# A Mamba stage whose first image is read before its weights

## The chip, the cores and the metric

The kernel runs on one core of a Trainium2 chip. Its engines work side by side, each through its own queue in order: TensorE (PE) multiplies matrices, VectorE (DVE) and GpSimd (POOL) work on tiles element by element, ScalarE (ACT) evaluates functions, and SyncE (SP) issues the DMA transfers between HBM and on-chip memory. Instructions on different engines wait for each other by semaphores. The metric is the device time of one execution in microseconds; lower is better. "Granted clock" is the share of TensorE's full clock that the throttle let through, by the profile.

## The reference, cut to what matters

Two layers, each added to its input: a Mamba block on group-normalised input, then an attention block on group-normalised input. The input x is 2 images of 256 channels with 64 x 64 positions, all float32. Layer 0, which the change is about:

```
x  = x + L0(gn(x))                      # gn: 32 groups of 8 channels, mean and variance over channels and all positions
yn = layernorm over channels * gamma + beta
xm, z = split(yn @ W_in.T)              # 512 each
u  = silu(causal conv of 4 taps (xm) + conv_b)
proj  = u @ W_xp.T                      # 16 for dt, 16 for B, 16 for C
dt = softplus(proj_dt @ W_dt.T + b_dt);  A = -exp(A_log)
h  = exp(dt A) h + (dt u) B             # scan over 4096 positions, 512 x 16 states
ym = (sum(h C) + u D) * silu(z)
y2 = ym @ W_out.T + yn
y3 = gelu(y2 @ W1.T + b1) @ W2.T + b2 + y2
```

The group norm needs the statistics of a whole image before the first of its positions can be normalised. Layer 1 is attention with 8 heads over 4096 positions; the change doesn't touch it.

## The kernel before

`conv_preact_kernel` loads a few constants, runs `mamba_stage` for both images, then `attention_block` for each. Within the Mamba stage an image is cut into 8 tiles of 512 positions (T), so there are 16 tiles: tiles 0 to 7 are the first image's, 8 to 15 the second's. An image tile is 128 partitions x 2 x 512 float32, which is 512 KB.

For each tile there are three parts. `front(i)` loads the tile into a buffer of the ring `yn` (L459), applies the group norm with the image's scales (L457), takes the mean over channels on PE, centres on DVE (L471), squares on ACT (L474), takes the variance on PE, then its inverse root on ACT (L479, L480), scales on DVE (L488) and shifts on ACT (L492). Four convolutions follow (`conv`): a projection on PE, a copy on ACT (L540), the taps as matmuls on PE, a silu on ACT (L536). Then come the projection to dt, B and C, and `softplus`. All these matmuls are recorded at L403, the line of a helper. The loop of `step` does the scan: 32 steps for each tile, with products on POOL and DVE and scans on DVE (L721). `back(i)` does the output projection (L599) with `w_out` and the two-layer perceptron with `w_1` and `w_2`.

The group norm's statistics come from `first(b, t)`: a load of an image tile into ring `h` (L315), and two `bn_stats` on DVE (L321), one for each half of the channels. Ring `h` has 5 buffers and is also that of the scan's steps. `group_norm(b, k)` aggregates (L412), averages over groups with two small matmuls by `gmat` (L403), and takes an inverse root on ACT by Ln and Exp (L424, L425). These and the front's inverse root need ACT's table "exp", the convolution's silu the table "silu"; a change of table is a load on ACT (L234). PSUM tiles of the front and of the group norm share the ring `mm` of 3 buffers.

The order of the stage's instructions is worked out by `Plan` when the kernel is built. Each task has an engine, a due time, a cost, and for DMAs a time to landing. Whenever an engine is free in the plan's time, the ready task with the lowest due (plus 6 when ACT's table would change) that finds buffers is put next. A task is only considered when its due is at most 24 (HORIZON) beyond the earliest due still unstarted:

```
if task.ready <= now and task.due <= dues[oldest].due + HORIZON:
    rank = (task.due + (SWITCH if task.tables and table not in task.tables else 0), task.at)
    if (best is None or rank < best[0]) and self.room(task, now):
```

That order is emitted under `tc.manual_schedule()`, so each engine's queue holds it as planned, however long things take on the chip. Tile i has its dues around 32 i: its front from 32 i - 46 (the load) over -39 (centring), -35 (scaling), -33 + 4k (the convolutions) to -12; its steps from 32 i on.

```
for b in range(IMAGES):
    for t in range(NT):
        first(b, t, -60 + 10 * b)
for b in range(IMAGES):
    for k in range(KC):
        group_norm(b, k, -48 + 10 * b)
```

Ahead of the plan stands the preparation: SP issues the loads of all weights and small vectors, in the order of the code (L334, L329, L341, L347, L349), then `perm`, `W_dt` and `pick` into the three buffers of ring `yn`. DVE works them into constants: `neg_a` (L359), `diag_d` (L364), `taps` (L369), `w_dt` (L379, L380) and `pick` (L383). The framework may change the order of these within the preparation.

Of the kernel before, what the change touches and what calls it, by code (L numbers as in the profile page):

```python
# [11 lines left out]
F32 = mybir.dt.float32  # L12
# [7 lines left out]
P = 128  # L20
# [3 lines left out]
D = 32  # L24
# [77 lines left out]
class Plan:  # L102
# [26 lines left out]
    def add(self, engine, due, cost, emit, reads=(), writes=(), tables=(), lands=0.0):  # L129


        task = Plan.Task()
        task.engine, task.due, task.cost, task.emit = engine, due, cost, emit
        task.tables, task.lands, task.at = tables, lands, len(self.tasks)
        deps = set()
        reads, writes = list(self.keys(reads)), list(self.keys(writes))
        for key in reads:
            deps.add(self.writer.get(key))
        for key in writes:
            deps.add(self.writer.get(key))  # L140
            deps.update(self.readers.get(key, ()))
        for key in reads:
            self.readers.setdefault(key, []).append(task)
        for key in writes:
            self.writer[key], self.readers[key] = task, []
        deps -= {None, task}
        task.deps, task.behind = len(deps), []
        task.ready, task.start = 0.0, None
        for dep in deps:
            dep.behind.append(task)  # L150
        task.bufs = list({id(b): b for b, _ in reads + writes}.values())
        for buf in task.bufs:
            if buf.ring and not buf.left:
                buf.turn = buf.ring.asked
                buf.ring.asked += 1
            buf.left += 1
        self.tasks.append(task)
# [89 lines left out]
def mamba_stage(ctx, tc, xs, stats_out, consts, w, outs):  # L247
# [12 lines left out]
    nc = tc.nc  # L260
    ident, gmat, lnmat, eps_t = consts
    IMAGES = len(xs)
    C, L = xs[0].shape
    KC = C // P
    NT = L // T
    DI = w["conv_w"].shape[0]
    KD = DI // P
    R = w["W_dtT"].shape[0]
    NP = w["W_xpT"].shape[1]
    N = (NP - R) // 2  # L270
    HID = w["W1T"].shape[1]
    KH = HID // P
# [6 lines left out]
    NS = LOW + NP  # L279

    wp = ctx.enter_context(tc.tile_pool(name="l0w", bufs=1))
# [4 lines left out]
    def ring(name, bufs, n=1, pool=None, rows=P, dtype=F32, free=False):  # L286
        return Ring(pool or sb, [rows, T] if n == 1 else [rows, n, T], name, bufs, dtype, free)

    mm = ring("mm", 3, pool=ps, free=True)
    r_yn, r_u, r_z = ring("yn", 3, KC), ring("u", KD + 1), ring("z", KD)  # L290
# [7 lines left out]
    r_h, r_y = ring("h", 5, 2), ring("y", 1, pool=ps)  # L298
# [5 lines left out]
    add = plan.add  # L304

    def image_tile(x, t):
        return x.rearrange("(k p) l -> p k l", p=P)[:, :, bass.ts(t, T)]


    stats_in = [wp.tile([P, KC, NT, nc.vector.BN_STATS_DIM], F32, name=f"stats_in{b}") for b in range(IMAGES)]  # L310
    stats_bufs = [Buf(parts=KC * NT, tile=s) for s in stats_in]

    def first(b, t, due):
        xt = Buf(r_h)
        add("SP", due, 0.8, lambda: nc.sync.dma_start(xt.tile, image_tile(xs[b], t)), [], [xt], lands=3.0)  # L315
        for k in range(KC):
            add(
                "DVE",
                due,
                0.7,  # L320
                lambda k=k: nc.vector.bn_stats(stats_in[b][:, k, t, :], xt.tile[:, k, :]),  # L321
                [xt],
                [stats_bufs[b][k * NT + t]],
            )


    def load_rows(name, src, k):
        t = wp.tile([P, k, src.shape[1]], F32, name=name)
        nc.sync.dma_start(t, src.rearrange("(k p) f -> p k f", p=P))  # L329
        return t  # L330

    def load_vec(name, src, k):
        t = wp.tile([P, k], F32, name=name)
        nc.sync.dma_start(t, src.rearrange("(k p) -> p k", p=P))  # L334
        return t

    gamma = load_vec("gamma", w["gamma"], KC)
    beta = load_vec("beta", w["beta"], KC)
    w_in = load_rows("w_in", w["W_inT"], KC)
    conv_w = wp.tile([P, KD, TAPS], F32, name="conv_w")  # L340
    nc.sync.dma_start(conv_w, w["conv_w"].rearrange("(k p) o t -> p k (o t)", p=P))  # L341
    conv_b = load_vec("conv_b", w["conv_b"], KD)
    w_xp = load_rows("w_xp", w["W_xpT"], KD)
    b_dt = load_vec("b_dt", w["b_dt"], KD)
    d_vec = load_vec("d_vec", w["D"], KD)
    neg_a = wp.tile([P, KD, QUAD, NQ], F32, name="neg_a")
    nc.sync.dma_start(neg_a, w["A_log"].rearrange("p (k j q) -> p k j q", k=KD, j=QUAD))  # L347
    sum4 = wp.tile([P, PQ], F32, name="sum4")
    nc.sync.dma_start(sum4, w["sum4"])  # L349
    w_out = load_rows("w_out", w["W_outT"], KD)  # L350
    w_1 = load_rows("w_1", w["W1T"], KC)
    b_1 = load_vec("b_1", w["b1"], KH)
    w_2 = load_rows("w_2", w["W2T"], KH)
    b_2 = load_vec("b_2", w["b2"], KC)


# [1 line left out]
    nc.scalar.activation(neg_a, neg_a, AF.Exp)  # L358
    nc.vector.tensor_scalar_mul(neg_a, neg_a, -1.0)  # L359
    diag_d = wp.tile([P, KD, P], F32, name="diag_d")  # L360
    perm = r_yn.make()[:, 0, 0:P]
    nc.sync.dma_start(perm, w["perm"])
    for k in range(KD):
        nc.vector.tensor_scalar_mul(diag_d[:, k, :], perm, d_vec[:, k : k + 1])  # L364

# [6 lines left out]
    w_dt = wp.tile([NS, 2, DI], F32R, name="w_dt")  # L372
    nc.gpsimd.memset(w_dt.bitcast(F32), 0.0)
    pick = wp.tile([NS, NQ, P], F32R, name="pick")
    w_dt32 = r_yn.make()[:R, 0, :]
    nc.sync.dma_start(w_dt32, w["W_dtT"])
    for row in (0, LOW):
        rows = slice(row, row + R)
        nc.vector.tensor_copy(w_dt[rows, 0, :], w_dt32)  # L379
        nc.vector.tensor_sub(w_dt[rows, 1, :], w_dt32, w_dt[rows, 0, :].bitcast(F32))  # L380
    pick32 = r_yn.make()[:NS, 0, :]
    nc.sync.dma_start(pick32, w["pick"])
    nc.vector.tensor_copy(pick.rearrange("r q p -> r (q p)"), pick32)  # L383

    projs = [wp.tile([NS, T], F32R, name=f"proj{i}") for i in range(2)]
    for t in projs:
        nc.gpsimd.memset(t.bitcast(F32), 0.0)
    r_proj.make = itertools.cycle(projs).__next__

# [9 lines left out]
    def matmul(out, pairs):  # L401
        for i, (lhsT, rhs) in enumerate(pairs):
            nc.tensor.matmul(out, lhsT=lhsT, rhs=rhs, start=(i == 0), stop=(i == len(pairs) - 1))  # L403

    def group_norm(b, k, due):

        s = Buf(r_gn)
        p1, p2 = Buf(mm), Buf(mm)
        out = scales_buf[b * KC + k]

        def aggregate():
            nc.vector.bn_aggr(s.tile[:, 0:2], stats_in[b][:, k, :, :].rearrange("p a s -> p (a s)"))  # L412

        def spread():


            nc.vector.tensor_copy(s.tile[:, 2:3], p1.tile[:, 0:1])
            nc.vector.tensor_sub(s.tile[:, 3:4], s.tile[:, 0:1], s.tile[:, 2:3])
            nc.vector.scalar_tensor_tensor(
                s.tile[:, 4:5], s.tile[:, 3:4], s.tile[:, 3:4], s.tile[:, 1:2], ALU.mult, ALU.add  # L420
            )

        def root():
            nc.scalar.activation(s.tile[:, 5:6], p2.tile[:, 0:1], AF.Ln, bias=eps_t)  # L424
            nc.scalar.activation(scales[:, b, k, 1:2], s.tile[:, 5:6], AF.Exp, scale=-0.5)  # L425

        def shift():
            nc.vector.scalar_tensor_tensor(
                scales[:, b, k, 0:1], s.tile[:, 2:3], -1.0, scales[:, b, k, 1:2], ALU.mult, ALU.mult
            )  # L430

        add("DVE", due, 0.4, aggregate, [stats_bufs[b][k * NT + t] for t in range(NT)], [s])
        add("PE", due, 0.4, lambda: matmul(p1.tile[:, 0:1], [(gmat, s.tile[:, 0:1])]), [s], [p1])
        add("DVE", due, 0.6, spread, [p1], [s])
        add("PE", due, 0.4, lambda: matmul(p2.tile[:, 0:1], [(gmat, s.tile[:, 4:5])]), [s], [p2])
        add("ACT", due, 0.6, root, [p2], [s, out], ("exp",))
        add("DVE", due, 0.2, shift, [s], [out])
# [325 lines left out]
            add("DVE", g + 2.5, 0.7, lambda: nc.vector.tensor_mul(d.z[k].tile, y.tile, d.z[k].tile), [y], [d.z[k]])  # L763

    for b in range(IMAGES):
        for t in range(NT):
            first(b, t, -60 + 10 * b)
    for b in range(IMAGES):
        for k in range(KC):
            group_norm(b, k, -48 + 10 * b)  # L770
    front(0)
    for i, d in enumerate(tiles):
        d.z, d.b, d.c, d.dt_rep, d.dtu_rep = [], [], [], {}, {}
# [482 lines left out]
```

## Time and profile before

| | us |
|---|---|
| median of 4 runs | 4627.26 (4626.51 to 4631.47) |
| the profiled execution | 4622.42 |
| its span, first to last instruction | 4620.6 |
| busy: PE, DVE, ACT, POOL | 4309.9, 3651.8, 3687.3, 3905.1 |
| first image load issued (L315, SP) | 15.91 |
| first and last of the 32 statistics (L321, DVE), starts | 22.8, 44.4 |
| first aggregation (L412, DVE) | 45.03 |
| first scaling in front 0 (L488, DVE) | 58.38 |
| first scan (L721, DVE) | 109.74 |

The granted clock over the span is 0.974. The page of the profile gives busy times over the whole span and in 40 slices; the timeline gives single instructions with their start and length in microseconds, and in brackets how long the engine stood idle before them and what ended that; "x10" after an instruction means that ten like it follow each other and are merged. A line with "SPq" is an instruction of SP's queue that issues a DMA: its length is the issue, not the transfer. The chain that ended last is found backwards from the last instruction, from each to what released it.

### The profile page before, as it was taken

How to read it: one execution, taken by the hardware profiler on the slowest of the kernel's cores; microseconds unless marked ns; L12 is line 12 of the kernel's file. 1: busy time of each engine (PE TensorE's matmuls, PEld its weight loads, DVE VectorE, ACT ScalarE, POOL GpSimd, SP SyncE). 2: the span in 40 equal slices, each digit the busy share in tenths (PEclk: the TensorE clock that was granted, in tenths of full speed). 3: DMA queues.
4: the chain of work that ended last, by engine and by line, in shares of the span. 5: the costliest groups of instructions: out<-in, count | busy, mean ns of one | idle time of the engine just before them, and what ended most of it. 6: DMA issues, size and time to landing. Idle time of an engine off the chain costs nothing.

```text
span 4620.6 us, 55923 instructions
## 1 busy us (share of the span) xinstructions
PE 4309.9 (93%) x18530; PEld 1569.5 (34%) x18530; DVE 3651.8 (79%) x3916; ACT 3687.3 (80%) x4860; POOL 3905.1 (85%) x2283
## 2 busy tenths in 40 slices
PE   4799899999999999888999999999989999999998
PEld 2233333333333333324333333333343333333332
DVE  3999999999999999964777767777747777777776
ACT  3788888888888888742888888888838888888887
POOL 1999999999999999960888888888818888888887
PEclk9899999999999999989999999999999999999999
DMA  5333333333333333308210140101081110401000
GB/s 174 105 111 110 103 122 121 122 124 124 124 124 123 111 119 124 114 33 266 66 44 17 26 99 19 26 17 26 10 266 33 44 26 19 99 17 26 23 25 8
DMA packets 162330, 379.67 MB, mean 82 GB/s; under 512 B 23408, under 2 KB 41584, under 8 KB 153840
## 3 DMA queue, kind: packets, MB, share of 16 engines
q1 hardware_dynamic: 162032, 376.03, 26.4%
q8 instruction: 147, 2.41, 0.2%
q14 instruction: 151, 1.24, 0.1%
HBM read 282.64 MB, written 93.32 MB: 81 GB/s over the span
## 4 chain that ended last, share of the span: by engine, by line
PE 64%; POOL 12%; DVE 10%; issue 6%; DMA 4%; ACT 3%; SPq 1%; POOLq 0%; DVEq 0%; ACTq 0%
PE s L963 27%; PE po L986 22%; PE mm L403 6%; DVE h L721 6%; POOL h L727 6%; POOL dbu L716 3%; PE y L753 2%; DMA xn<-x_dram 2%; PE mm L599 2%; PE mm L635 1%; PE s L887 1%; DVE bn L716 1%; PE bn L403 1%; ACT L234 1%; POOL lw L572 1%
## 5 line engine op out<-in xcount | busy, mean ns | idle before, releaser
L977 ACT ACTIVATE e<-s 128x1024 f32<-128x1024 f32 x2048 | 1987.6, 1023 | 284.5 <-PE s L963 281.7
L1007 DVE TENSOR_TENSOR acc<-acc,e 128x1024 f32<-128x1024 f32 x992 | 1220.0, 1230 | 566.4 <-ACT e L977 563.3
L1018 POOL TENSOR_TENSOR acc_p<-acc_p,e 128x1024 f32<-128x1024 f32 x544 | 1299.3, 2388 | 228.2 <-ACT e L977 214.8
L963 PE MATMUL s<-q,k 128*128 128x512 f32 x4096 | 1321.5, 436 | 12.9 <-ACT e L977 10.0
L727 POOL TENSOR_TENSOR h<-h,c 128x1024 f32<-128x1024 f32 x512 | 1205.7, 2369 | 16.3 <-ACT state L724 11.0
L986 PE MATMUL po<-e,v 128*32 128x512 f32 x8192 | 1093.8, 605 | 0.0
L963 PEld LDWEIGHTS s<-q,k 128*128 128x128 f32 x4096 | 615.8, 188 | 1131.5 <-ACT e L977 1123.0
L710 ACT ACTIVATE da<-dt_rep,neg_a 128x512 f32<-128x512 f32 x1024 | 691.7, 701 | 122.4 <-DVE h L721 100.9
L721 DVE TENSOR_TENSOR_SCAN h<-da,state,dbu 128x512 f32<-128x512 f32 x512 | 649.8, 1274 | 80.4 <-POOL dbu L716 70.9
L721 DVE TENSOR_TENSOR_SCAN h<-da,state,bn 128x512 f32<-128x512 f32 x512 | 647.5, 1265 | 13.7
L1016 POOL TENSOR_TENSOR acc_p<-acc_p,e 128x512 f32<-128x512 f32 x416 | 533.7, 1283 | 32.7 <-POOL acc_p L1018 0.2
L716 POOL TENSOR_TENSOR dbu<-dtu_rep,b 128x512 f32<-128x512 f32 x384 | 487.4, 1281 | 10.5 <-DMA dtu_rep<-dtu_dram 9.1
L234 ACT ACT_TABLE_LOAD x331 | 424.7, 1283 | 6.5 <-PEq L1246 0.7
L753 PE MATMUL y<-h,sum 128*32 128x512 f32 x2048 | 380.5, 641 | 41.3 <-POOL h L727 41.3
L403 PE MATMUL bn<-proj,pick 112*128 112x512 f32 x512 | 306.4, 614 | 118.8 <-DVE h L721 118.3
L716 DVE TENSOR_TENSOR bn<-dtu_rep,bn 128x512 f32<-128x512 f32 x512 | 348.7, 681 | 34.4 <-PE bn L403 17.2
L1009 POOL TENSOR_TENSOR acc_p<-e 128x1024 f32<-128x1024 f32 x32 | 76.4, 2388 | 270.6 <-ACT e L977 270.6
L986 PEld LDWEIGHTS po<-e,v 128*32 128x32 f32 x8192 | 161.6, 108 | 375.0 <-issue 361.7
L403 PE MATMUL mm<-yn,w_in 128*128 128x512 f32 x512 | 262.7, 638 | 10.0 <-ACT yn L492 4.5
L1015 DVE TENSOR_TENSOR acc<-acc,e 128x512 f32<-128x512 f32 x384 | 264.8, 690 | 0.0
L403 PE MATMUL mm<-xm,taps 128*128 128x512 f32 x512 | 235.6, 603 | 15.8 <-POOL xm L539 13.6
L403 PE MATMUL mm<-yn,w 128*128 128x512 f32 x512 | 239.1, 596 | 11.5 <-ACT z L587 10.3
(126 smaller groups left out, 3470.1 us busy)
## 6 DMA issues: line engine op xcount, KB each, us to landing
dt_rep<-dt_dram SPq DMA_DIRECT2D x128, 512.0 KB, 5.3
dtu_rep<-dtu_dram SPq DMA_DIRECT2D x128, 512.0 KB, 5.8
qk_dram<-halves SPq DMA_DIRECT2D x64, 512.0 KB, 5.7
q<-qk_dram SPq DMA_DIRECT2D x128, 256.0 KB, 4.7
k<-qk_dram SPq DMA_DIRECT2D x64, 512.0 KB, 7.4
b<-bc_dram SPq DMA_DIRECT2D x64, 256.0 KB, 3.0
c<-bc_dram SPq DMA_DIRECT2D x64, 256.0 KB, 4.0
dt_dram<-dt SPq DMA_DIRECT2D x64, 256.0 KB, 2.0
```

Source lines behind the costliest of these rows:

```text
L403: nc.tensor.matmul(out, lhsT=lhsT, rhs=rhs, start=(i == 0), stop=(i == len(pairs) - 1))
L710: nc.scalar.activation(da[j].tile, dt.tile[:, j, :], AF.Exp, scale=scale)
L716: engine.tensor_mul(out.tile, dtu.tile[:, j, :], rows.tile)
L721: nc.vector.tensor_tensor_scan(h.tile[:, j, :], da[j].tile, dbu.tile, initial, ALU.mult, ALU.add)
L727: nc.gpsimd.tensor_tensor(h.tile, h.tile, rows_c.tile.unsqueeze(1).to_broadcast([P, 2, T]), ALU.mult)
L753: nc.tensor.matmul(y.tile[j * PQ : (j + 1) * PQ, :], lhsT=sum4, rhs=pair[j // 2].h.tile[:, j % 2, :], start=False, stop=(qd == NQ - 1),)
L963: nc.tensor.matmul(ps[:, j, :], lhsT=keys[i // NT, kt][:, h, kj : kj + P], rhs=queries[i][:, h, :], start=True, stop=True,)
L977: nc.scalar.activation(e, d.s[half], AF.Exp, scale=SCALE)
L986: nc.tensor.matmul(tiles[i].po[h * D : (h + 1) * D, :], lhsT=v[:, c, g * P + h * D : g * P + (h + 1) * D], rhs=todo[s].e[h // 2][:, h % 2, :],
L1007: nc.vector.tensor_add(acc, acc, ea)
L1016: nc.gpsimd.tensor_add(acc_p[:, 1, :], acc_p[:, 1, :], eb[:, 1, :])
L1018: nc.gpsimd.tensor_add(acc_p, acc_p, eb)
```

## The change

The first image's statistics leave the plan. They are emitted directly, ahead of all weights: for each of the 8 tiles the load and its two `bn_stats`, in a scheduled block of their own. The second image's stay in the plan with due -30 instead of -50, and the group norms have dues -48 and -24 instead of -48 and -38.

The loads of the weights come in another order: those that the first front uses first, with `W_dt`, `pick` and `perm` among them rather than at the end; `w_in` moves behind the small convolution vectors. `W_dt` and `pick` now take the first two buffers of ring `yn` and `perm` the third. The three matrices that only `back` uses, `w_out`, `w_1` and `w_2` (512 KB, 1 MB and 1 MB), are loaded by a task of the plan on SP with due -20.

```diff
     def first(b, t, due):
         xt = Buf(r_h)
-        add("SP", due, 0.8, lambda: nc.sync.dma_start(xt.tile, image_tile(xs[b], t)), [], [xt], lands=3.0)
+        load = lambda: nc.sync.dma_start(xt.tile, image_tile(xs[b], t))
+        stats = lambda k: nc.vector.bn_stats(stats_in[b][:, k, t, :], xt.tile[:, k, :])
+        if b == 0:
+
+            xt.tile = r_h.make()
+            load()
+            for k in range(KC):
+                stats(k)
+            return
+        add("SP", due, 0.8, load, [], [xt], lands=3.0)
         for k in range(KC):
...
+            add("DVE", due, 0.7, lambda k=k: stats(k), [xt], [stats_bufs[b][k * NT + t]])
+
+    with tc.manual_schedule():
+        for t in range(NT):
+            first(0, t, 0)
...
     gamma = load_vec("gamma", w["gamma"], KC)
     beta = load_vec("beta", w["beta"], KC)
-    w_in = load_rows("w_in", w["W_inT"], KC)
     conv_w = wp.tile([P, KD, TAPS], F32, name="conv_w")
     nc.sync.dma_start(conv_w, w["conv_w"].rearrange("(k p) o t -> p k (o t)", p=P))
     conv_b = load_vec("conv_b", w["conv_b"], KD)
+    w_in = load_rows("w_in", w["W_inT"], KC)
     w_xp = load_rows("w_xp", w["W_xpT"], KD)
     b_dt = load_vec("b_dt", w["b_dt"], KD)
-    d_vec = load_vec("d_vec", w["D"], KD)
     neg_a = wp.tile([P, KD, QUAD, NQ], F32, name="neg_a")
     nc.sync.dma_start(neg_a, w["A_log"].rearrange("p (k j q) -> p k j q", k=KD, j=QUAD))
+    w_dt32 = r_yn.make()[:R, 0, :]
+    nc.sync.dma_start(w_dt32, w["W_dtT"])
+    pick32 = r_yn.make()[:NS, 0, :]
+    nc.sync.dma_start(pick32, w["pick"])
+    d_vec = load_vec("d_vec", w["D"], KD)
+    perm = r_yn.make()[:, 0, 0:P]
+    nc.sync.dma_start(perm, w["perm"])
     sum4 = wp.tile([P, PQ], F32, name="sum4")
     nc.sync.dma_start(sum4, w["sum4"])
-    w_out = load_rows("w_out", w["W_outT"], KD)
-    w_1 = load_rows("w_1", w["W1T"], KC)
     b_1 = load_vec("b_1", w["b1"], KH)
-    w_2 = load_rows("w_2", w["W2T"], KH)
     b_2 = load_vec("b_2", w["b2"], KC)
...
+    late_buf = Buf()
+
+    def load_late():
+        for tile_, name in ((w_out, "W_outT"), (w_1, "W1T"), (w_2, "W2T")):
+            nc.sync.dma_start(tile_, w[name].rearrange("(k p) f -> p k f", p=P))
...
     for b in range(IMAGES):
-        for t in range(NT):
-            first(b, t, -60 + 10 * b)
+        for t in range(NT if b else 0):
+            first(b, t, -30)
     for b in range(IMAGES):
         for k in range(KC):
-            group_norm(b, k, -48 + 10 * b)
+            group_norm(b, k, -48 + 24 * b)
+    add("SP", -20, 2.4, load_late, [], [late_buf], lands=12.0)
     front(0)
```

More of the change, by code (lines that the diff above doesn't have):

```diff
@@ L314, in first @@
         xt = Buf(r_h)
-        add("SP", due, 0.8, lambda: nc.sync.dma_start(xt.tile, image_tile(xs[b], t)), [], [xt], lands=3.0)
-        for k in range(KC):
[L317 to L324, printed above, removed]
+        load = lambda: nc.sync.dma_start(xt.tile, image_tile(xs[b], t))
[7 more added lines that the diff above has]
+        add("SP", due, 0.8, load, [], [xt], lands=3.0)
+        for k in range(KC):
+            add("DVE", due, 0.7, lambda k=k: stats(k), [xt], [stats_bufs[b][k * NT + t]])
+    with tc.manual_schedule():
+        for t in range(NT):
+            first(0, t, 0)
     def load_rows(name, src, k):
@@ L360, in mamba_stage @@
     diag_d = wp.tile([P, KD, P], F32, name="diag_d")
-    perm = r_yn.make()[:, 0, 0:P]
-    nc.sync.dma_start(perm, w["perm"])
     for k in range(KD):
@@ L374, in mamba_stage @@
     pick = wp.tile([NS, NQ, P], F32R, name="pick")
-    w_dt32 = r_yn.make()[:R, 0, :]
-    nc.sync.dma_start(w_dt32, w["W_dtT"])
     for row in (0, LOW):
@@ L380, in mamba_stage @@
         nc.vector.tensor_sub(w_dt[rows, 1, :], w_dt32, w_dt[rows, 0, :].bitcast(F32))
-    pick32 = r_yn.make()[:NS, 0, :]
-    nc.sync.dma_start(pick32, w["pick"])
     nc.vector.tensor_copy(pick.rearrange("r q p -> r (q p)"), pick32)
@@ L388, in mamba_stage @@
     r_proj.make = itertools.cycle(projs).__next__
+    w_out, w_1, w_2 = (
+        wp.tile([P, k, C if name != "w_1" else HID], F32, name=name)
+        for name, k in (("w_out", KD), ("w_1", KC), ("w_2", KH))
+    )
+    late_buf = Buf()
+    def load_late():
+        for tile_, name in ((w_out, "W_outT"), (w_1, "W1T"), (w_2, "W2T")):
+            nc.sync.dma_start(tile_, w[name].rearrange("(k p) f -> p k f", p=P))
     state = wp.tile([P, IMAGES, KD, QUAD, NQ], F32, name="state")
```

## The prediction

> **What bounds the kernel now.** I read the page first: the 4620.6 us span is the Mamba stage (to about 2040 us) and two attention blocks. Of the 40 slices below (115.5 us each), POOL is at 9 tenths in all of the Mamba part but the first slice, and the first slice is where all the engines are least busy.
>
> ```profile
> span 4620.6 us, 55923 instructions
> PE   4799899999999999888999999999989999999998
> DVE  3999999999999999964777767777747777777776
> ACT  3788888888888888742888888888838888888887
> POOL 1999999999999999960888888888818888888887
> ```
>
> A table of windows then gives the state once the Mamba loop runs, and the rate of the image loads in the opening (columns: window and length, busy time of PE, weight loads, DVE, ACT and POOL, granted clock, DMA share, GB/s). POOL works 198.69 of 200 us, so the loop is bound by POOL, and time won ahead of the loop moves everything behind it. The loads run at 384 to 391 GB/s at a DMA share of about 1: the queue is full.
>
> ```profile
> 28.00:32.00 4.00, 0.00 (x0) 0.00 (x0) 2.72 (x5) 0.00 (x0) 0.00 (x0) 1.00 1.06 391
> 32.00:36.00 4.00, 0.00 (x0) 0.00 (x0) 3.74 (x7) 0.00 (x0) 0.00 (x0) 1.00 1.05 384
> ...
> 700.00:900.00 200.00, 186.18 (x562) 70.58 (x561) 186.63 (x204) 167.94 (x278) 198.69 (x130) 0.97 0.41 138
> ```
>
> The timeline of DVE, 0 to 60 us, shows what the opening consists of (start, length, line, operation). Tap matrices and other constants end at 22.9 us, held back by a load that lands at 19.38; then come 32 statistics of both images, to 45.1; then the group norm; the first front's centring at 53.40 and scaling at 58.38.
>
> ```profile
> 9.70 1.46 DVE L369 TENSOR_SCALAR taps<-ident,conv_w 128x128 f32<-128x128 f32 x7
> 19.38 0.87 DVE L364 TENSOR_SCALAR diag_d<-yn,d_vec 128x128 f32<-128x128 f32 x4 [8.21 <-DMA yn<-in_perm]
> 20.16 0.86 DVE L379 CAST w_dt<-yn 16x512 fp32r<-16x512 f32 x2
> 22.83 6.03 DVE L321 BATCH_NORM_STATS2 stats_in<-h 128x6 f32<-128x512 f32 x10
> 30.07 6.76 DVE L321 BATCH_NORM_STATS2 stats_in<-h 128x6 f32<-128x512 f32 x10 [1.22 <-DMA h<-in_x]
> 37.05 8.06 DVE L321 BATCH_NORM_STATS2 stats_in<-h 128x6 f32<-128x512 f32 x12 [0.23 <-DMA h<-in_x]
> 45.03 0.58 DVE L412 BATCH_NORM_AGGREGATE gn<-stats_in 128x2 f32<-128x48 f32 x2
> 53.40 1.29 DVE L471 TENSOR_TENSOR yn<-yn,mm 128x512 f32<-128x512 f32 x2 [3.01 <-PE mm L403]
> 58.38 1.41 DVE L488 SCALAR_TENSOR_TENSOR yn<-yn,gamma,mm 128x512 f32<-128x512 f32 x2 [3.56 <-ACT mm L480]
> ```
>
> The same on SP's queue: no image load is issued before 15.91, behind all weights, and the front's own tile (L459) goes out at 20.28, when the constants let go of its buffer.
>
> ```profile
> 14.46 0.47 SPq L362 DMA_DIRECT2D yn<-in_perm  x1
> 15.91 3.89 SPq L315 DMA_DIRECT2D h<-in_x  x5
> 20.28 0.37 SPq L459 DMA_DIRECT2D yn<-in_x  x1
> 24.13 14.61 SPq L315 DMA_DIRECT2D h<-in_x  x11
> ```
>
> Last the chain that ended last, 0 to 125 us: these pieces all lie on it, so the opening is serial, and one PE run of 27.86 us carries the rest of the front.
>
> ```profile
> 14.46 4.89 DMA yn<-in_perm
> 24.13 5.92 DMA h<-in_x
> 45.11 0.28 DVE gn L412
> 59.94 27.86 PE mm L403 x60
> 88.90 1.28 ACT L234
> ```
>
> **The first image's statistics ahead.** Eight loads of 512 KB start at 1.20 us instead of 15.91. The small gamma load lands 2.1 us after issue; a 0.524 MB tile at 388 GB/s takes 1.35 us, so the first lands near 4.6 and the eighth near 14.1. SP must wait for the first tile's two statistics before load six, but these end near 6 while five loads cover DMA to 10: no hole. The statistics (16 x 0.68 = 10.9 us) end about 15.5.
>
> **Weights in order of need.** On SP the 15 small and front weights now queue behind load eight, which waits for the third tile's statistics (about 8.7). At 0.5 us each they are issued by about 16.5. By the differences of successive landings in the trace (W_in about 2.8 us, conv_w 0.4, conv_b 0.5, w_xp 0.25, b_dt 0.25, A_log 0.3, W_dt 0.25, pick 0.65, d_vec 0.2, perm 0.25, gamma and beta 0.3) they land between 14.1 and 20.3 us. DVE's constants, formerly under the loads, now lie behind the statistics: taps 3.3, neg_a 0.2, w_dt 0.86 + 1.40, pick 0.43, diag_d 0.87, together 7.1 us from 15.5: 22.6 if nothing waits, 24 if diag_d precedes w_dt and waits for perm. I take 23.0 for the aggregation against 45.03: 22.0 us early. The three temporary loads now take the ring of yn in another order, so the front's tile waits for w_dt: issued at 21.4 to 23.4, I take 22.0, landed about 25.5, just ahead of its use at 26.2 (aggregate to norm took 48.27 - 45.03 = 3.24).
>
> **Second image's statistics beside the front.** I followed the planner by hand with its own costs. At planner time 0 the group norm and the front's tile go first; SP then places second-image loads 1 to 5 (ring h has five buffers). At 5.6 the first group norm has started in full, the horizon of 24 opens to due -20, load 6 still has no buffer: so the three late weights go out **between load 5 and load 6**. DVE gets six statistics before the centring (ready 8.95), and seven more, those of tiles 4 to 6 and half of tile 7, before the scaling (ready 15.3): fillers, by the planner's landing of 3 us. Every one stands in DVE's in-order queue, and behind them stands the scaling, and behind that ACT's shift and the 60 matmuls.
>
> On the chip the queue from the front's tile to load 7 holds 0.524 + 5 x 0.524 + 0.524 + 1.049 + 1.049 + 2 x 0.524 = 6.82 MB. At 385 GB/s that is 17.7 us; the landings of w_out (3.8 us) and W2 (3.4 behind its predecessor) say some 1.1 more for their narrow rows; 2 us to the first bytes. From 22.0: tile 7 at 42.8, its statistic to 43.5. Without that wait the scaling would be ready at 23.0 + (58.38 - 45.03) = 36.4, with the centring undelayed (six statistics done about 31.5 against 31.4). The new wait is thus about 7.1 us, bounded by 0 (another order) and 11 (order and rate both bad). The scaling comes at 43.5 instead of 58.38: **14.9 us early**. At the 358 GB/s per core that the Trainium skill, "DMA: Bandwidth & Descriptors", Specifications, states for HBM, the 6.82 MB would take 19.0 us and the gain would be 13.6, an estimate by that page alone. The trace's 384 to 391 GB/s disagrees, so I keep the row.
>
> **Second group norm inside the front's PE run.** Its due goes from -38 to -24, between the third projection and the third convolution of front 0. Eight matmul records of such a norm: 16 took 3.9 us in the opening, so at most 1.95 us, at least half of that. The PSUM ring mm has three buffers, so the fourth projection waits for the third silu: 0.3 to 1. Its Ln and Exp need another table: a load of 1.28 us before, one after; the second is in ACT's idle time, the first can hold back the copy of the fourth projection, which lets the second front's mean and variance matmuls (1.98) move ahead of the projection that was earlier in front of them. Against that the table load and L479/L480 after 88.9 (1.28 + 0.66 + 0.58) may leave the chain. Together I estimate 3.0 us lost, between 2 gained and 6 lost. The same norm's matmuls also leave the mean's neighbourhood (some 0.7 us), but that lies ahead of the new wait and is worth nothing.
>
> **The rest.** Late weights are used first behind a whole tile's loop (L599), over 100 us later: hidden. DVE's second-image statistics cost 10.9 us in a gap; DVE was idle from 60 to 84, so nothing beyond the wait above. The loop and attention are the same work. No trace of before shows whether the planner's altered start reorders the loop: I take 0, bounded by 3 us either way, since POOL can gain at most the 1.3 idle us per 200.
>
> **Sum.** 14.9 - 3.0 = 11.9 us. The profiled execution took 4622.42 us (span 4620.6 and 1.8 around it), so 4610.5 against it. The runs' median is 4627.26, 4.84 above the profiled one; the change is the same there: 4627.26 - 11.9 = **4615.4**.
>
> **Rivals.**
> Late weights hidden: the scaling isn't held back, because the queue order differs or the other fillers come elsewhere. For: DVE had 24 idle us in the old front. Against: the W2 load that took 9.3 us shows that large loads queue. Gain 58.38 - 36.4 - 3.0 = 19.0, time 4608.3.
> Constants late: SP's queue showed one stall of 4.02 us behind many small loads. If it falls between the weights and the front's tile together with a wait for perm, all of the opening is some 6 us later: gain 6, time 4621. Against: the weights land in time with DVE free only at 15.5.
> Slower: the loop's order slips. The place is the POOL queue in the 16 tile loops, its price any extra idle: before it is 1.3 per 200, about 0.8 per tile of 120.7 us. It decides when a tile loses 11.9/16 = 0.74 us more; at 1.5 more, 24 - 12 = 12 us are lost, 4639. Against: dues of all loop tasks are untouched. For: the window 300 to 500 shows 8.3 idle us, so POOL can be starved.
>
> **How the numbers follow.** Chances: forecast 0.55, late weights hidden 0.20, constants late 0.15, slower loop 0.10. 0.2% is 9.3 us, about what a measurement of this kernel can tell. The forecast's own range, 14.9 (12 to 18) less 3 (-2 to 6), is 4608 to 4621; it is over 9.3 in three quarters of the cases. Faster: 0.55 x 0.75 + 0.20 = 0.61; slower 0.10; the rest 0.29. The range takes in the hidden case with some of its gain in the front (4605), and constants late with a bad front (4624).
>
> **What would show it.** First image load on SP at about 1.2 us; aggregation near 23; L599's weights issued between the fifth and sixth load of the second image; DVE waiting on an image load for some 7 us ahead of L488, which starts near 43.5; the PE run of front 0 some 31 us long with L403 matmuls of gmat in it; the first scan at 98 instead of 109.74; the loop's POOL idle unchanged. I am wrong if L488 starts near 36 or beyond 47, or if the opening is won and the time not.

## The result, and the profile after

The changed kernel takes 4620.24 us (median of 32 runs) against 4626.91 us (52 runs of the kernel before beside them): ratio 0.9987, 95% interval 0.9982 to 0.9992. By the ratio that is 6.0 us won, between 3.7 and 8.3 (the plain difference of the medians is 6.7), where 11.9 were forecast. The time lies in the stated range, 4605 to 4624; of the prediction's classes it falls into "within 0.2%", which had a chance of 0.29, and not into "faster", which had 0.61.

The two profiled executions can't show this by their ends: 4622.60 us after, 4622.42 before. The kernel before happened to be 4.5 us under its own median, and the attention blocks, whose code and order no edit touches, took from 2579.7 to 2588.6 us in the profiles of this study (from the last product with C to the end of the span). So below, single profiles are read for the opening and the Mamba loop, and medians for the time.

The page's head, and lines of DVE's timeline over the opening (start, length, line, operation; in brackets the idle time before it and what ended that). Most lines of the changed kernel are 15 further down in the code: L486 is the centring, L503 the scaling, L418 the helper for matmuls. The statistics are at L316, and L403 is now the load of the late weights.

```profile
span 4621.1 us, 55917 instructions
```

```profile
14.97 1.29 DVE L316 BATCH_NORM_STATS2 stats_in<-h 128x6 f32<-128x512 f32 x2 [0.39 <-DMA h<-in_x]
16.17 0.58 DVE L427 BATCH_NORM_AGGREGATE gn<-stats_in 128x2 f32<-128x48 f32 x2
16.67 3.15 DVE L377 TENSOR_SCALAR taps<-ident,conv_w 128x128 f32<-128x128 f32 x16
23.21 1.39 DVE L386 TENSOR_TENSOR w_dt<-yn,w_dt 16x512 fp32r<-16x512 f32 x2
33.82 1.27 DVE L486 TENSOR_TENSOR yn<-yn,mm 128x512 f32<-128x512 f32 x2
35.01 2.46 DVE L316 BATCH_NORM_STATS2 stats_in<-h 128x6 f32<-128x512 f32 x4
43.77 2.05 DVE L316 BATCH_NORM_STATS2 stats_in<-h 128x6 f32<-128x512 f32 x3 [6.30 <-DMA h<-in_x]
45.74 1.39 DVE L503 SCALAR_TENSOR_TENSOR yn<-yn,gamma,mm 128x512 f32<-128x512 f32 x2
```

The first image's statistics end at 16.3 (45.1 was the end of all 32 before), and the first aggregation follows at once, ahead of the constants. Then DVE stands for 6.30 us at a statistic of the second image; two more statistics and then the scaling stand behind it. The scaling comes at 45.74 instead of 58.38.

SP's queue shows why that statistic had to wait: the three late weights (L403; `W1T`, issued at 28.27, is not among the lines) stand between loads 5 and 6 of the second image.

```profile
1.20 8.38 SPq L315 DMA_DIRECT2D h<-in_x  x8
24.63 0.37 SPq L474 DMA_DIRECT2D yn<-in_x  x1
25.04 2.68 SPq L315 DMA_DIRECT2D h<-in_x  x5
27.76 0.47 SPq L403 DMA_DIRECT2D w_out<-in_W_outT  x1
29.06 0.49 SPq L403 DMA_DIRECT2D w<-in_W2T  x1
31.30 6.10 SPq L315 DMA_DIRECT2D h<-in_x  x3
```

Lines of PE's timeline show the rest of the first front. Before, it was one run of 27.86 us.

```profile
47.28 5.37 PE L418 MATMUL mm<-yn,w_in 128*128 128x512 f32 x8 [10.09 <-ACT yn L507]
52.48 7.03 PE L418 MATMUL mm<-xm,taps 128*128 128x512 f32 x16
61.06 0.50 PE L418 MATMUL mm<-gn,gmat 128*128 128x1 f32 x4
65.46 0.50 PE L418 MATMUL mm<-gn,gmat 128*128 128x1 f32 x4
66.40 1.98 PE L418 MATMUL mm<-yn,w_in 128*128 128x512 f32 x4 [0.44 <-ACT u L551]
68.22 1.88 PE L418 MATMUL mm<-yn,lnmat 128*128 128x512 f32 x4
73.37 1.88 PE L418 MATMUL mm<-tmp,lnmat 128*128 128x512 f32 x4
75.09 1.88 PE L418 MATMUL mm<-yn,w_in 128*128 128x512 f32 x4
76.90 3.63 PE L418 MATMUL mm<-u,w_xp 128*48 128x512 f32 x8
```

From 47.28 to the end of the last projection at 80.53 are 33.25 us. The second norm's matmuls take twice 0.50. Behind them the second front's variance (73.37) and the projection of a gate (z in the reference, 75.09) stand ahead of the first front's last projection (76.90); in the kernel before both came after it.

ACT's timeline has five loads of a function table between the third silu and the first softplus (L568); before there was one, at 88.90.

```profile
66.36 1.28 ACT L234 ACT_TABLE_LOAD   x1
72.11 1.28 ACT L234 ACT_TABLE_LOAD   x1
74.28 1.28 ACT L234 ACT_TABLE_LOAD   x1
76.86 1.28 ACT L234 ACT_TABLE_LOAD   x1
84.86 1.28 ACT L234 ACT_TABLE_LOAD   x1
86.16 0.69 ACT L568 ACTIVATE dt<-mm,b_dt 128x512 f32<-128x512 f32 x1
```

Where the 12.6 us went, from the two profiles (us; each is the start of that instruction):

| | before | after | earlier by |
|---|---|---|---|
| scaling in front 0 | 58.38 | 45.74 | 12.6 |
| copy of the projection to dt, B, C | 87.82 | 80.57 | 7.3 |
| first softplus | 91.38 | 86.16 | 5.2 |
| first scan | 109.74 | 105.13 | 4.6 |
| last product with C, the loop's end | 2039.1 | 2035.6 | 3.5 |

So 8.0 us go between the scaling and the first scan, nearly all of them before the first softplus: 5.4 on PE up to the copy of the projection and 2.0 between that copy and the softplus.

### The profile page after: what moved, and what is told of

It is laid out like the page before. It is cut to its first block, busy times and chain, and to the rows that moved or that the text cites. A ratio compares the mean times of both kernels' runs of the same rounds, so it can differ in the third digit from the quotient of the medians.

```text
span 4621.1 us, 55917 instructions
## 1 busy us (share of the span) xinstructions
PE 4317.8 (93%) x18530; PEld 1573.7 (34%) x18530; DVE 3651.6 (79%) x3916; ACT 3690.1 (80%) x4861; POOL 3910.2 (85%) x2283
## 4 chain that ended last, share of the span: by engine, by line
PE 57%; POOL 11%; DVE 10%; issue 6%; ACT 6%; DMA 3%; SPq 0%; ACTq 0%; POOLq 0%; DVEq 0%
PE s L979 25%; PE po L1002 20%; DVE h L736 6%; POOL h L742 6%; PE mm L418 4%; POOL dbu L731 3%; ACT e L993 2%; PE y L768 2%; PE mm L614 1%; PE mm L650 1%; PE s L903 1%; ACT da L725 1%; ACT L234 1%; DVE bn L731 1%; DMA xn<-x_dram 1%
## 5 line engine op out<-in xcount | busy, mean ns | idle before, releaser
L418 PE MATMUL bn<-proj,pick 112*128 112x512 f32 x512 | 308.4, 617 | 126.9 <-DVE h L736 126.6
L731 DVE TENSOR_TENSOR bn<-dtu_rep,bn 128x512 f32<-128x512 f32 x512 | 348.7, 681 | 33.3 <-DMA dtu_rep<-dtu_dram 18.9
L418 PE MATMUL mm<-yn,w_in 128*128 128x512 f32 x512 | 260.6, 635 | 14.0 <-ACT yn L507 10.6
L418 PE MATMUL mm<-yn,w 128*128 128x512 f32 x512 | 240.8, 599 | 12.4 <-ACT z L602 11.1
L418 PE MATMUL mm<-xm,taps 128*128 128x512 f32 x512 | 236.1, 604 | 15.4 <-POOL xm L554 12.6
```

The source lines that it names most:

```text
L731: engine.tensor_mul(out.tile, dtu.tile[:, j, :], rows.tile)
```

## The experiments

The theory after the result had two costs inside the opening: the late weights in the image loads' queue, and the second image's norm in the first front. Against each stood the rival that it is covered by something else, and against both that the loop's planned order decides. The edits of e5 and e6 are made to the kernel before, all others to the changed kernel; each ratio is against the kernel before on the same chip. e1 keeps the planned orders of PE, DVE, ACT and POOL of the changed kernel, and e10 and e8 those of e7 with due -11, so within these pairs only transfers move. Each checkpoint (scaling, first scan, loop's end) is from a single profile. e3 and e9 have the same orders of PE, DVE, ACT and POOL up to the second norm, and still differ by 1.2 us at the scaling and 2.4 at the first scan: in e9 the four matmuls of the first front's variance take 3.78 us, in e3 1.98, with a granted clock of 1.00 in both. Why isn't shown. So a checkpoint is good to some 2 us.

| | time, us | ratio (95%) | scaling | first scan | loop's end |
|---|---|---|---|---|---|
| changed kernel | 4620.24 | 0.9987 (0.9982 to 0.9992) | 45.7 | 105.1 | 2035.6 |
| e1 late weights behind | 4615.44 | 0.9978 (0.9969 to 0.9987) | 39.4 | 98.7 | 2028.9 |
| e2 norm at 196 | 4627.41 | 1.0002 (0.9993 to 1.0011) | 46.2 | 99.9 | 2043.8 |
| e3 both | 4620.28 | 0.9989 (0.9980 to 0.9998) | 39.4 | 93.0 | 2036.2 |
| e4 both, buffers | 4618.53 | 0.9984 (0.9975 to 0.9993) | 37.5 | 91.7 | 2033.2 |
| e5 first image alone | 4625.20 | 0.9996 (0.9987 to 1.0005) | 57.6 | 111.3 | 2044.4 |
| e6 second image alone | 4621.95 | 0.9990 (0.9981 to 0.9999) | 48.5 | 107.5 | 2032.0 |
| e7, norm at -11 | 4607.90 | 0.9960 (0.9947 to 0.9974) | 40.7 | 91.0 | 2020.9 |
| e7, norm at -6 | 4612.25 | 0.9970 (0.9958 to 0.9982) | 40.0 | 94.5 | 2025.2 |
| e10 norm alone at -11 | 4613.75 | 0.9970 (0.9959 to 0.9981) | 46.0 | 96.2 | 2027.3 |
| e8 norm at -11, buffers | 4610.53 | 0.9954 (0.9940 to 0.9967) | 37.2 | 86.9 | 2020.8 |
| e9 norm at 100 | 4619.42 | 0.9980 (0.9970 to 0.9991) | 40.6 | 95.4 | 2034.2 |

**The late weights.**

```diff
-    add("SP", -20, 2.4, load_late, [], [late_buf], lands=12.0)
+    add("SP", -13, 2.4, load_late, [], [late_buf], lands=12.0)
```

> Only the three late weights' due goes from -20 to -13, which puts them on SP's queue behind all eight loads of the second image and the front's next tile; the orders of PE, DVE and ACT stay those of the changed kernel. Theory (the 2.62 MB of late weights between load 5 and 6 hold up DVE's queue): the 6.3 us wait of DVE for an image load goes, the first scaling comes at about 38.8 us instead of 45.74 (33.82, the centring, plus the 4.98 that separate the two in the kernel before), the first scan at about 98 instead of 105.13, and the time is about 7 us below the changed kernel's. Rival (the wait is covered by something else downstream): the scaling moves, the first scan by less than 3 us, the time by less than 2. Rival (late weights were not the cause, the image loads themselves are slow): the scaling moves by less than 2 us.

The timeline of DVE in this kernel, the stretch that answers to 35.01 to 45.74 above:

```profile
35.26 4.24 DVE L316 BATCH_NORM_STATS2 stats_in<-h 128x6 f32<-128x512 f32 x7
39.42 1.39 DVE L503 SCALAR_TENSOR_TENSOR yn<-yn,gamma,mm 128x512 f32<-128x512 f32 x2
```

The seven statistics run without a break and the scaling follows at 39.42, 6.3 us earlier; the first scan is 6.4 earlier, the loop's end 6.7. The median is 4.8 lower (4620.24 - 4615.44; 4.2 by the ratios), less than the 7 expected, and by the time alone the two intervals overlap; it is the checkpoints that show the gain. The wait was the late weights', and all of it was on the path up to the loop's end.

**The second norm, away from the front.**

```diff
-            group_norm(b, k, -48 + 24 * b)
+            group_norm(b, k, 8 * STEPS - 60 if b else -48)
```

> Only the second image's group norm changes its due, from -24 to 196, six tiles later; its statistics stay where they are. Theory (the norm inside the front's PE run costs through the planner's order: matmuls of the second front and of a gate slip ahead of the first front's last projection, and a table load more): the scaling stays at 45.7 us, the time from the first convolution's projection (47.28) to the copy of the projection (80.57) falls from 33.3 us to about 29, the first softplus from 86.16 to about 81, the first scan from 105.13 to about 101; the time is about 4 us below the changed kernel's. Rival (the loss in the front is PE's clock or the ring mm, not the norm): the same 33 us. Rival (the loop's order, which this moves too, decides): the scan comes earlier and the time does not follow.

> Both edits: late weights behind the second image's loads, its group norm six tiles later. If the two costs are separate they add: scaling at 38.8 us, first scan near 94, time about 11 us below the changed kernel's and 17 below the kernel before. If the front is bound by something else once one of them is gone, the gain is that of the larger alone, about 7.

The front did what the theory says: in e2 the time from the first projection to the copy of the projection fell from 33.3 us to 27.8, the first softplus came at 82.41, and with the norm away the first scan came 5.2 us earlier (e2 against the changed kernel) and 5.7 earlier (e3 against e1). That is not all of the 8.0: from the scaling to the first scan e2, e3 and e5, none of which has the norm there, take 53.6 to 53.7 us, the kernel before 51.4. ACT's timeline of e3 shows a gate's activation (L602) ahead of the first softplus, between two more table loads; before, the gates came at 99.73, behind the first two softplus tasks:

```profile
69.58 1.28 ACT L234 ACT_TABLE_LOAD   x1
72.16 1.28 ACT L234 ACT_TABLE_LOAD   x1
73.46 0.60 ACT L602 ACTIVATE z<-mm 128x512 f32<-128x512 f32 x1
74.07 1.28 ACT L234 ACT_TABLE_LOAD   x1
75.37 0.69 ACT L568 ACTIVATE dt<-mm,b_dt 128x512 f32<-128x512 f32 x1
```

The time did not follow: 4627.41 and 4620.28 are 7.2 and 4.8 us above their neighbours, and the rival that the loop decides was right about the time. The times between the back stores of successive tiles show where (us, from SP's issues of x_dram):

```
before: 123.6 123.7 120.7 120.7 120.7 120.7 120.7 120.7 120.8 120.7 120.7 120.7 120.7 116.4
after:  125.2 123.9 120.8 120.8 120.8 120.8 120.8 120.8 120.8 120.8 120.8 121.0 120.8 117.2
e3:     120.6 124.3 122.6 120.3 138.3 119.1 120.9 120.7 120.7 120.7 120.7 120.7 120.6 116.5
e9:     120.6 137.9 120.0 120.9 120.7 120.7 120.7 120.7 120.7 120.7 120.7 120.7 120.6 116.3
```

One tile of e3 takes 138.3 us instead of 120.7. The norm ran just ahead of and in it, at 779 to 860 us. The timelines of DVE and POOL there:

```profile
831.68 0.13 DVE L432 COPY gn<-mm 128x1 f32<-128x1 f32 x1
831.84 2.01 DVE L433 TENSOR_TENSOR gn<-gn 128x1 f32<-128x1 f32 x1
833.88 6.03 DVE L434 SCALAR_TENSOR_TENSOR gn<-gn 128x1 f32<-128x1 f32 x1
839.84 0.36 DVE L427 BATCH_NORM_AGGREGATE gn<-stats_in 128x2 f32<-128x48 f32 x1
```

```profile
838.63 1.26 POOL L588 TENSOR_TENSOR dt<-dt,lw 128x512 f32<-128x512 f32 x1
843.44 2.36 POOL L742 TENSOR_TENSOR h<-h,c 128x1024 f32<-128x1024 f32 x1 [3.55 <-ACT state L739]
```

An instruction on 128 x 1 elements, 0.22 us in the opening, holds DVE for 6.03 us; the scans stand behind it, and POOL then idles 3.55 us for lack of a scanned tile. More was lost later in the same tile, at 931 to 951, where SP's and ACT's queues waited for transfers. Whether that was the norm's doing or that of the place where the second image begins is what the last run asked:

> As the third kernel (late weights behind the second image's loads, second norm late), but the norm's due is 100 instead of 196, in the fourth tile's loop instead of the seventh's. In the third kernel one tile, between the back stores at 812.6 and 951.0, took 138.3 us instead of 120.7, with the norm at 779 to 860 and SP's and ACT's queues held up at 931 to 951, where the second image's first front begins. Theory (the norm's own tasks in the full loop cost the time): the long tile moves with the norm, to between about 445 and 700 us. Rival (the order of the plan where the second image begins costs it, whatever the norm): the long tile stays at 812 to 951. The first scan stays at 93 in both.

The edit is the due, 100 for 196. The long tile moved with the norm (411 to 496 us), to the tile between 448.3 and 586.2, and the place where the second image begins took its usual 120.7. The first scan, expected at 93, came at 95.4. So the norm's own tasks in the full loop lengthen one tile by some 17 us, in both places tried. Part of that comes back elsewhere: from its first product with C to its last the loop takes 1939.5 us in e3 and 1934.7 in e9, against 1927.4 in e1, so 12.1 and 7.3 more. How the 6.03 us turn into 17 by way of the planned order isn't resolved further.

**Buffers for the constants.**

```diff
-    w_dt32 = r_yn.make()[:R, 0, :]
+    w_dt32 = r_h.make()[:R, 0, :]
...
-    pick32 = r_yn.make()[:NS, 0, :]
+    pick32 = r_h.make()[:NS, 0, :]
...
-    perm = r_yn.make()[:, 0, 0:P]
+    perm = r_h.make()[:, 0, 0:P]
```

> As the third kernel, and the three temporary constants (W_dt, pick, perm) land in buffers of ring h instead of ring yn, so that the front's own tile no longer waits on SP for DVE's w_dt. Theory (DMA is idle from 19.5 to 25 us because SP's queue stands at that load, L474 at 24.63): the load goes out near 21.2, the centring comes near 30.5 instead of 33.8, the scaling near 35.5, the first scan some 3.3 us earlier than in the third kernel, and the time 3 us lower. Rival (the constants on DVE set the pace up to 25.8): the scaling moves by less than 1 us.

The scaling moved 1.9 us, the first scan 1.3, against 3.3 expected: between the two stated cases. The centring moved 2.5 us, and the scaling then waited 0.47 us for the variance, whose four matmuls took 3.16 us here and 1.98 in e3. The time, 1.7 us lower, is within the intervals. The same edit on the best order, below, tells more.

**One part of the change alone.** The kernel before with only the first image ahead of the weights (`first` itself as in the change):

```diff
+    with tc.manual_schedule():
+        for t in range(NT):
+            first(0, t, 0)
...
-        for t in range(NT):
-            first(b, t, -60 + 10 * b)
+        for t in range(NT if b else 0):
+            first(b, t, -50)
```

> The kernel before with one part of the change alone: the first image's loads and statistics stand ahead of the weights; weights, second image's statistics (due -50) and group norms (-48, -38) as before. Theory (the gain of the opening is the second image's statistics leaving it, more than the first's going ahead): the first aggregation can come near 16 us, but the constants wait for perm behind 4.2 MB of weights, near 31, and the front's tile goes out after that and behind five loads of the second image; the scaling comes near 50, 8 us before the 58.4 of the kernel before, and as the second norm stays out of the front the first scan gains the same 8; time about 8 us below before. Rival (the first image ahead is the whole of the gain): scaling near 45.

The aggregation came at 16.32, but the constants waited 8.40 us for perm and the second image's statistics ran from 33.98 to 45.61, ahead of the front:

```profile
16.32 0.59 DVE L418 BATCH_NORM_AGGREGATE gn<-stats_in 128x2 f32<-128x48 f32 x2
30.54 0.87 DVE L370 TENSOR_SCALAR diag_d<-yn,d_vec 128x128 f32<-128x128 f32 x4 [8.40 <-DMA yn<-in_perm]
33.98 6.22 DVE L316 BATCH_NORM_STATS2 stats_in<-h 128x6 f32<-128x512 f32 x10
```

The scaling is at 57.6, 0.8 us earlier where 8 were expected, because those statistics are in front of the scaling whatever comes first; the first scan is at 111.3, 1.6 later than before, and the time isn't to be told from the kernel before. The other part, the second image's dues alone:

```diff
-            first(b, t, -60 + 10 * b)
+            first(b, t, -30 if b else -60)
...
-            group_norm(b, k, -48 + 10 * b)
+            group_norm(b, k, -48 + 24 * b)
```

> The kernel before with the other part alone: dues of the second image's statistics -30 instead of -50 and of its norm -24 instead of -38; the first image still behind all weights. Theory: 16 statistics of 0.68 leave the way of the first norm, so the scaling comes some 9 to 11 us earlier, near 48; of that the norm inside the front's PE run takes 5.7 (the first scan of 98.7 with it there against 93.0 with it away), so the first scan comes near 105 instead of 109.7; time about 3 to 5 us below before. Rival (the two parts need each other): scaling later than 54.

The scaling came at 48.5, 9.9 us earlier, as expected; the first scan at 107.5, only 2.2 earlier (some 5 expected), since the front lost 7.7 and not 5.7. Its ratio, 0.9990, is not to be told from the 0.9987 of the whole change. The loop's end came 7.1 us earlier, more than the first scan: in this order the loop takes 1921.8 us instead of 1925.5. The second image's dues alone bring most of what the change wins. The rest of the change adds 2.8 us at the scaling, and it would add 9.1 if the late weights, which it moves into the plan, stood behind the image loads (48.5 here, 39.4 in e1).

**A better place for the second norm.** With the late weights behind the image loads, due -11 and due -6:

```diff
-            group_norm(b, k, -48 + 24 * b)
+            group_norm(b, k, -11 if b else -48)
```

> Late weights behind the second image's loads, and the second image's group norm with due -11 instead of -24: it now stands around the first front's last projection, after all four silus, and takes the table that the softplus needs next. Theory (the norm's cost in the front, 5.7 us, is the two table changes and the matmuls that slip ahead of the last projection, and its cost in the loop, 12 us, is that of engines that are full): here neither is paid; the first scan comes near 94 instead of the 98.7 of the first experiment, the loop keeps its 1927 us, and the time is some 4 to 5 us below that experiment's. Rival (any other order of the plan moves the loop by more than that): first scan near 94 and the time not below.

> The same with due -6: the norm falls among the first softplus tasks, its table the one in use; the second front's mean and variance go as in the kernel whose norm is late (e3). Theory: first scan near 94 to 95, loop 1927, time as in the kernel with due -11 within 2 us. Rival (the loop's order is touchy at its start): the two kernels differ by more than 3 us, and the difference lies in the first tiles of the loop.

ACT's timeline for due -11 shows the norm's roots under the table that the softplus needs anyway:

```profile
68.88 0.58 ACT L531 CAST proj<-mm 48x512 fp32r<-48x512 f32 x1 [3.31 <-PE mm L418]
69.96 1.28 ACT L234 ACT_TABLE_LOAD   x1
71.25 0.26 ACT L439 ACTIVATE gn<-mm,eps_t 128x1 f32<-128x1 f32 x1
72.04 0.67 ACT L568 ACTIVATE dt<-mm,b_dt 128x512 f32<-128x512 f32 x1
```

One table load stands between the projection and the softplus, and the roots cost 0.8 us there. The first scan is at 91.0, 7.7 us before e1's, and the loop, from the first product with C (94.7) to the last, takes 1926.2 us against 1927.4. At 4607.90 us, ratio 0.9960 (0.9947 to 0.9974), this is below the changed kernel beyond both intervals; e1's interval it touches at the edge, but its loop ends 8.0 us before e1's. The norm's price is not all that is saved: in e7 the second front's variance, its roots and the gates stand behind the first softplus, which comes 3.2 us after the copy of the projection instead of 6.9 in e3. So from the scaling to the first scan e7 takes 50.3 us, less than the 53.6 of e3, which has no norm there at all. With due -6 the first scan is 3.5 us later and the time 4.4 us higher; that is the size of the rival, but most of the difference is there before the loop, not in its first tiles. The expected 2 us were missed, and the rival was right in the size alone.

> The changed kernel with one edit, the second image's group norm at due -11 instead of -24; late weights stay between load 5 and 6. The orders of PE, DVE, ACT and POOL are those of the kernel with both edits (e7, due -11). Theory (the two costs are separate and add): scaling at 46 us as in the changed kernel, first scan near 97 instead of 105.1, time 6 to 8 us below the changed kernel's and some 5 above that of the kernel with both edits. Rival (the late weights' wait is hidden once the front is shorter): first scan near 91 and the time as with both.

With the norm's due alone changed, the changed kernel, e1, e10 and e7 make a square. Their runs were taken on different chips, where the medians of the kernel before lie between 4626.18 and 4629.25 us, so the ratios are compared: late weights behind are worth 4.2 us with the norm at -24 (0.9987 to 0.9978) and 4.6 with it at -11 (0.9970 to 0.9960); the norm's place is worth 7.9 and 8.3. At the loop's end it is 6.7 and 6.4 for the late weights, 8.3 and 8.0 for the norm's place. The two costs are separate and add, as far as intervals of 0.1% can tell for the time.

> The kernel with both edits (late weights behind, norm at due -11), and the three temporary constants in buffers of ring h, so that the front's tile does not wait on SP for w_dt. All five engines' orders stay the same. Theory: the scaling comes at about 38 instead of 40.7, the first scan at 88 to 90 instead of 91.0, the time some 2 us below that kernel's. Rival (the constants on DVE, to 25.8 us, set the pace): less than 1 us.

The edit of the constants' buffers on that kernel brought the scaling to 37.2 and the first scan to 86.9, 3.5 and 4.1 us earlier, more than expected. The loop gave it back: it takes 1930.9 us instead of 1926.2 and ends at 2020.8 against 2020.9. The orders of all engines are the same in both, so an earlier start of the loop isn't always kept; why is open. The times, 0.9954 and 0.9960, can't be told apart.

## Why the prediction was right, and where it was wrong

The direction, the mechanism of the gain and that of the new wait were right; the sum was about twice too large. At the first scan 4.6 us were won where 11.9 were forecast: 2.3 are missing at the scaling and 5.0 in the front. That 6.0 us is also what the rival "constants late" had forecast is chance, since its stall did not come.

- *What bounds the kernel.* Right for the late weights: 6.3 us at the scaling became 6.7 at the loop's end. The rule that the loop moves with its start isn't strict: without a norm in it the loop takes between 1921.8 us (e6) and 1930.9 (e8), and the profiles don't say why.
- *The first image's statistics ahead.* Right: first load at 1.20, statistics to 16.3 (15.5 forecast).
- *Weights in order of need.* The aggregation at 16.17, not 23.0: the framework didn't keep the preparation ahead of the plan here, and DVE did the norm between the constants. The front's tile was issued at 24.63 (22.0 forecast), when w_dt let go of its buffer, and with it began the queue of image loads that set the scaling. The step got the event right and its time 2.6 us too early. The centring came at 33.82 instead of 31.4. A smaller wait of the same kind as the new one lies ahead of it, which the prediction did not have: the statistic at 29.92 waited 4.07 us for its load, the scale of the second half of the channels (30.53) stood behind it, and ACT idled 1.32 us for that scale.
- *The wait behind the late weights.* Right in place, size and cause: 7.1 us forecast, 6.30 seen, 6.3 gone with the late weights moved. The scaling came 12.6 us early, not 14.9; the missing 2.3 are put down to the front's tile, 2.6 us late. The queue moved at 349 to 394 GB/s in the windows from 26 to 46 us, around the row that the sum used. By the 358 of the Trainium skill, "DMA: Bandwidth & Descriptors", Specifications, the queue would have been slower than in three of these five windows (394, 389 and 387).
- *The second group norm inside the front.* This is the term that failed. 3.0 us were forecast, 6 as the worst; from the scaling to the first scan it took 8.0 more (59.4 against 51.4), and the first scan came at 105.13 instead of 98. The pieces were named, but the matmuls that move ahead were counted as one pair (1.98) where a gate went ahead too (1.88), and one table load held back where there were five; the softplus, 3.6 us behind the projection's copy before, was 5.6 behind it after. Of the 8.0 the norm itself costs 5.7, since the stretch takes 53.7 us with it away (e2): near the bound, not beyond it. The other 2.3 are there without the norm too, with the gate's activation and its table loads ahead of the first softplus; the prediction had no such change of order. With the norm at -11, where the second front's variance and the gates stand behind the first softplus as well, the stretch takes 50.3 us.
- *The loop.* 0 within 3 us forecast; 1927.7 against 1925.5 us in the profiles, 2.2 lost, most of it in the first tile (125.2 against 123.6).
- *Rivals.* Late weights were not hidden. "Constants late" did not come as told: DVE's constants end at 25.85 us, later than the 22.6 to 24 of the forecast, but no load held them up: the norm's instructions stand between them. The change itself lost 2.2 us in the loop, within the 3 allowed; e2, with another due, has one tile 18 us longer, so a loop can be disturbed in this way.

## What to carry to other kernels

Work moved "beside" a stage by a planner stands in in-order queues there: what decides is which transfer the filler waits for and which instruction stands behind it, so cold loads belong behind the loads that fillers wait for. Tiny tasks are cheap only where their engine's state suits them: the same norm cost 5.7 us between two silus and 7 to 12 over the full loop, while under the table that the next stage needs its roots took 0.8. Follow a gain by checkpoints (here scaling, first scan, loop's end) before the total, since one execution's total varied by more than the gain.

## What the runs showed of the hardware

VectorE instructions on 128 x 1 elements with two SBUF inputs took 0.16 and 0.22 us in the opening, with POOL idle. In e3's loop five of the six took 1.13 to 6.03 us, one 0.15; the copies beside them, whose input is in PSUM, took 0.13 and 0.15. Each of the five ends within 0.06 us of the end of a POOL instruction. The 6.03 us end at 839.91, where POOL's row of four back-to-back instructions ends too (833.89 to 839.89). The scans of the loop, which have one of their two large inputs in PSUM, keep to 1.25 to 1.28 us beside a busy POOL (300 to 700 us). The Trainium skill, "SBUF — State Buffer", section "SBUF: two separate sides", says that VectorE with two SBUF inputs and GpSimd share a port pair under an exclusive lock, held for the whole instruction. That agrees with the 2.01 us, which end with one POOL instruction (831.44 to 833.80); that the wait can last over four of them is more than that section says. No run here takes POOL's work away to prove it.
